# The sums of a block in two steps, and two loads of x asked for first, in a graph kernel with sorted edges

## The chip, the cores and the metric

The kernel runs on one core of a Trainium2 chip. Its time is what the device takes for one execution, in microseconds (us), and the time given is a median over several executions. A profile is one execution taken by the hardware profiler. PE is TensorE (matrix products), PEld its loading of weights, DVE is VectorE, ACT is ScalarE, POOL is GpSimd, SP is SyncE. SP, ACT and POOL also issue transfers (DMAs); on POOL these are the gathers, whose rows are picked by a list of indices.

## What is computed

One layer of a graph network over 12,500 nodes with 128 features and 412,500 edges, which come sorted by their target `dst`. Cut to what matters:

```python
theta = x[dst] - x[src]
w = sigmoid(relu(theta @ W1 + b1) @ W2 + b2)
agg = segment_sum(w * theta, dst)          # per node
indeg = segment_sum(1, dst)                # edges per node
y = x + agg + indeg * (x @ W4 + b4)
out = layernorm(y)                         # over the 128 features, no weights
```

Every edge has a gate `w` between 0 and 1. A node's result is the sum of its edges' gated differences, the number of its edges times a linear map of its own row, its own row, and a normalization.

## The kernel before

**The table.** Since `(x[dst] - x[src]) @ W1` is a difference of two rows of `x @ W1`, the kernel first makes a table `z` in DRAM whose rows are `x @ W1` and `x` side by side, 256 numbers. It does so in 14 chunks of up to 1024 rows: `table_load` (L726 to L731) asks for a chunk of x on ACT's queue, `table_chunk` (L734) turns it on PE (L743), copies it on ACT (L746), multiplies it by W1 (L749), copies that (L752) and x (L753) into a buffer, and SP writes the buffer to `z` (L754). Loads run up to two chunks ahead of the chunk worked on (`chunk`, L1243). The first two chunks are put behind `place_first_src` (L463), which turns the first list of `src` (load L164, copy L458, product L460, copy L464): `with after([first])` orders their instructions behind it.

**The sorting.** Edges are handled in parts of about 1400. For each set of parts a long generator, `place` (L481 on), sorts the edges of every part into places, most of it on DVE, and yields now and then, so that its steps can be spread between other work. It starts from the lists `es` and `ed` (SP's loads, L182) and ends with a list of rows to gather, `src_i`, copied by ACT (L687). The first set's loads are issued on SP near the start, and its steps are spread over the table's chunks and the first parts.

**A part and a block.** There are 300 parts (`s`), two to a block (`b`), 150 blocks; a block's targets lie in a window of 96 nodes. For part `s`:

- `gather(s)`: 8 gathers of 128 rows of `z` each, on POOL (L382), into one of 7 buffers (`zbuf`).
- `spread_y(s)`: products on PE that give each edge its target's row of `x @ W1` (L871). Later `y` tiles alternate between two.
- `logits(s)`, on DVE: subtract (L929), relu times W2 (L934), sum (L940), and the one-hot matrix of targets `ow` (L904).
- `open_gate`, `gate_sums` and `weigh`: the gate on ACT (L946, L952), then the gated rows `wx`, half on DVE (L974), half on ACT (`weigh_rest`, L981).

A few edges of each part, the "hot" ones, have their rows fetched in another way, by products with tables held in SBUF (`products_of_tiles`, L1035; `hot_rows(b)`, L1075 and L1079; `hot_logits`, L1088; `hot_weights`, L1099).

**The sums of a block.** `sums_of(b)` starts a tile in PSUM, `pa`, of which there is one, with the node's own part (L1132, L1133) and turns the next window (L794). `add_block(b)` (L1152) calls it and then adds on PE, all in `pa` (L1121): four wide products (260 columns) of the even part, four of the odd part, six narrow ones (130 columns) of the hot edges, and one that carries over the sums of the block before. `total(b)` copies parts of `pa` on ACT (L1169, L799), `finish(b)` adds the rest on DVE (L1180); `own` (L1188, L1190) and `normalize` (L1208 to L1233) make the output.

**The order of the work.** From part 18 on the order on PE, DVE and ACT is the order of the calls in `part(s)` (L1436 on). The queue of SP is in program order too; POOL's gathers follow one another in order. In `part(s)`, with `h` the part's number in its block, `logits(s)` comes first, then `spread_ahead(s)`, which issues `spread_y(s + 2)` and `gather(s + 3)`. That gather has a pace:

```python
paced[s + 3] = newest[0]
gather(s + 3)
```

`newest[0]` is the last product that `hot_rows`, `hot_products` or `products` put on PE, and the first of the part's gathers waits for it. With `h == 0` follows `add_block(b - 1)`, then in both parts `products_of_tiles`; with `h == 1` follows `hot_rows(b + 1)`. So the newest product before an even part is the last of `hot_rows`, and before an odd part the last of `products_of_tiles`. `total(b - 1)` and `finish(b - 1)` come with `h == 1`.

Of the kernel before, what the change touches and what calls it, by code (L numbers as in the profile page):

```python
# [81 lines left out]
def gnn_resnorm(  # L82
# [78 lines left out]
    def load_first(edges, s0, m):  # L161

        t = early(P, I32)[:m * K]
        nc.sync.dma_start(  # L164
            t, edges[s0 * BE:(s0 + m) * BE].rearrange("(p e) -> p e", e=P))
        return t
# [55 lines left out]
    load_bases(0, FIRST)  # L222
    wts = const.tile([P, 2, D], F32, name="wts")
    nc.sync.dma_start(wts[:, 0, :], W1)
    dst_f = load_first(dst, 0, FIRST)
    loaded = load(0)
    load_bases(FIRST, PLAIN)
# [101 lines left out]
        return nodes, (apart, most, area_c)  # L329


    wx_buf = [const.tile([P, K, AW], F32, name=f"wx{i}") for i in range(NW)]
    wxh_all = const.tile([P, 2 * SUB * HQ, AW], F32, name="wxh")
    wxh_buf = [wxh_all[:, i * SUB * HQ:(i + 1) * SUB * HQ, :] for i in range(2)]
    xT_all = const.tile([P, HX, HK], F32, name="xT")
# [13 lines left out]
    def pairs(s):  # L349
        return J if s < NF else JT  # L350
# [10 lines left out]
    def wx_of(s):  # L361

        if s < NH:
            return wxe_buf[s % 2]
        return wx_buf[s % (EW if s < PLAIN else NW)]
# [327 lines left out]
    with tc.manual_schedule(engines={SP}), tc.tile_pool(name="work", bufs=2) as wp, tc.tile_pool(  # L693
# [28 lines left out]
        def turning():  # L722

            return ps_l.tile([P, P * G], F32, name="pd")

        def table_load(c):  # L726
            n0, np_, m = chunks[c]
            xt = wx_buf[c % EW].rearrange("p k d -> p (k d)")[:, :BE]
            xt = xt.rearrange("p (t d) -> p t d", d=D)
            nc.scalar.dma_start(  # L730
                xt[:np_, :m, :], x[n0:n0 + np_ * m, :].rearrange("(p t) d -> p t d", t=m))  # L731
            return xt

        def table_chunk(c, xt):  # L734

# [173 lines left out]
        def logits(s):  # L909

            zs = rows_of(s)
            lg = parts[s]["lg"] = wp.tile([P, K, 1], F32, name="lg")
            y = parts[s]["y"]
            if s < NH:
                one_hot_w(s)
                for i, h in enumerate(y):
                    w2 = w2_r.rearrange("p (o d) -> p o d", o=1).to_broadcast([P, J, D])
                    nc.vector.scalar_tensor_tensor(h, h, 0.0, w2, op0=OP.max, op1=OP.mult)
                    nc.vector.tensor_reduce(lg[:, i * J:(i + 1) * J, 0], h, AX.X, OP.add)
                return  # L920
            h = zs[:, :, :D]
            n = pairs(s)
            half = h.rearrange("p (i k) d -> p i k d", i=2)[:, :, :n, :]
            if s < PLAIN:
                for i in range(2):
                    nc.vector.tensor_sub(half[:, i], y[i], half[:, i])
            else:
                yy = y[0][:, :n, :].rearrange("p (o k) d -> p o k d", o=1)
                nc.vector.tensor_sub(half, yy.to_broadcast([P, 2, n, D]), half)  # L929
            w2 = w2_b.rearrange("p (o d) -> p o d", o=1)  # L930
            n = K if s < NF else JT
            tiles = [slice(i, i + n) for i in range(0, K, J if n < K else K)]
            for at in tiles:
                nc.vector.scalar_tensor_tensor(  # L934
                    h[:, at, :], h[:, at, :], 0.0, w2.to_broadcast([P, n, D]),
                    op0=OP.max, op1=OP.mult)
            if s % SUB == 0:
                one_hot_w(s)
            for at in tiles:
                nc.vector.tensor_reduce(lg[:, at, 0], h[:, at, :], AX.X, OP.add)  # L940
            if s % SUB:
                one_hot_w(s)
# [175 lines left out]
        def products(to, terms, first, last):  # L1118

            for i, (one, w) in enumerate(terms):  # L1120
                newest[0] = nc.tensor.matmul(to if len(w.shape) == 3 else to[:, 0, :], one, w,  # L1121
                                             start=first and i == 0, stop=last and i == len(terms) - 1)

        def sums_of(b):

            pa = ps_l.tile([P, P * G], F32, name="pa")
            d = blocks[b]
            d["pa"] = pa[:WB, :2 * AW].rearrange("p (h c) -> p h c", h=2)
            d["pau"] = pa[:WB, AW:2 * AW + D]
            d["turned"] = pa[:, 2 * AW + D:2 * AW + D + WB]  # L1130
            u = pa[:WB, 2 * AW:2 * AW + D]
            nc.tensor.matmul(u, third, b4_t, start=True, stop=False)  # L1132
            nc.tensor.matmul(u, d["xuT"], wts[:, 1, :], start=False, stop=True)  # L1133
            if b + 1 < NK:
                turn(b + 1, d["turned"])

        def add_up(s, halves=(0, 1)):
# [11 lines left out]
            if end:  # L1149
                parts.pop(s)  # L1150

        def add_block(b):  # L1152

            sums_of(b)
            d = blocks[b]
            terms = []
            for s in range(b * SUB, b * SUB + SUB):
                wx = wx_of(s).rearrange("p (h k) d -> p k h d", h=2)
                terms += [(parts[s]["ow"][0][:, k, :], wx[:, k]) for k in range(pairs(s))]
                parts.pop(s)  # L1160
            terms += [(d["owh"][:, q, :], d["wxh"][:, q, :]) for q in range(SUB * HQ)]
            terms.append((d["sh"][:WB, :WB], carry[0][:WB, :AW]))
            products(d["pa"], terms, True, True)

        def total(b):

            d = blocks[b]
            a = d["a"] = carry[0] = wp.tile([P, AW + D], F32, name="a", bufs=3)
            nc.scalar.activation(a[:WB], d["pau"], AF.Copy)  # L1169
            d["u"] = a[:WB, AW:]  # L1170
            if b + 1 < NK:
                turned(b + 1, d["turned"])

        def finish(b):

            d = blocks[b]
            a = d["a"]
            plain = b * SUB < PLAIN
            if not plain:
                nc.vector.tensor_add(a[:WB, :AW], a[:WB, :AW], d["pa"][:, 0, :])  # L1180
# [57 lines left out]
            if b < NK:  # L1238
                load_block(b)

        xts, done = [], []

        def chunk():  # L1243
            c = len(done)
# [27 lines left out]
        def advance(kinds, n=1):  # L1272

            for _ in range(n):
                if steps[0] is None or steps[1] not in kinds:
                    return
                steps[1] = next(steps[0], None)
                if steps[1] is None:
                    steps[0] = None
# [148 lines left out]
        def spread_ahead(s):  # L1428

            if s + 2 < NS:  # L1430
                spread_y(s + 2)
                if PLAIN + AHEAD <= s + 3 < NS:
                    paced[s + 3] = newest[0]
                    gather(s + 3)

        def part(s):  # L1436

            b, h = divmod(s, SUB)
            credit[0] = min(credit[0] + 2.1, 5.0)
            if s in turns:  # L1440
                edges[s + 3] = turns[s], load(turns[s])
            if s in edges:
                i, loaded = edges.pop(s)
                assert steps[0] is None
                steps[:] = place(i, lambda: where[0](), *loaded), "k"
            for f in rest_of:
                if f[0] - 8 == s:
                    hot_load(f)
            if h == 0:
                fetch(b + 2)  # L1450
            if s == PLAIN:
                normalize(b - 2)
            done_b = h == 1 and PLAIN // SUB - 1 <= b - 1 < NK
            while opened:
                hot_out(*opened.pop(0))
            if h == 1:
                advance("c")
            if s < NS:
                logits(s)
            spread_ahead(s)  # L1460
            if h == 0 and PLAIN // SUB <= b - 1 < NK:
                add_block(b - 1)
            if tiled:
                products_of_tiles()
            if h == 1 and b + 1 < NK:
                hot_rows(b + 1)
            if s < NS:
                open_gate(s)
            if done_b:
                total(b - 1)  # L1470
            if s < NS:
                if h == 0:
                    hot_logits(b)
                else:
                    shift(b)
                weigh(s)
            if done_b:
                finish(b - 1)
            if h == 1:
                spend("kz", 1)  # L1480
            if h == 0 and b < NK:
                hot_weights(b)
            if s < NS:
                gate_sums(s)
            if done_b:
                own(b - 1)
            if s < NS:
# [215 lines left out]
```

## Time and profile before

| | us |
|---|---|
| median of 3 runs | 3143.19 (3138.27 to 3147.16) |
| the profiled execution | 3137.42 |
| its span | 3135.6 |
| PE, DVE, POOL, ACT busy | 2627.0, 2597.9, 2305.1, 2158.6 |
| POOL's gathers from `z` | 2250 by `src_i`, 112 by the first list |

The page gives, for each engine, its busy time and the number of instructions. A line of a group reads: line of the kernel, engine, operation, output and inputs, shapes, count, then busy time in us and the mean of one in ns, then the idle time of the engine just before these instructions, and what ended most of it. "issue" means that the engine waited for nothing that the profile shows. A line of the waits reads: engine, line and tile that waited, what for, us in total, how often, the longest. A line of the timeline reads: start and length in us, engine, line, operation, tiles, how many were merged, and in brackets the idle time before it with what ended it. A line of the stretches reads: from and to, length, busy us and count of PE, PEld, DVE, ACT and POOL, the clock granted to PE, the busy share of the DMA engines, and GB/s.

### The profile page before, as it was taken

The numbers are of one execution on the slowest core, as the hardware profiler recorded it, in microseconds if no ns is written. First come the engines' busy times: TensorE is split into PE (matmuls) and PEld (weight loads), VectorE is DVE, ScalarE is ACT, GpSimd is POOL, SyncE is SP. The second block draws the span as 40 slices with busy tenths as digits, with TensorE's granted clock in tenths as the row PEclk, the third lists the DMA queues.
The fourth block names the chain that finished last, engine by engine and source line by source line (L and its number), as shares of the span: only waits on it lengthen the run. The fifth ranks groups of instructions, "written<-read, shape, count | busy, mean of one in ns | idle before, by whom it ended". The sixth has DMA issues, their size and how long they took to land.

```text
span 3135.6 us, 52391 instructions
## 1 busy us (share of the span) xinstructions
PE 2627.0 (84%) x14981; PEld 2127.1 (68%) x14981; DVE 2597.9 (83%) x5715; ACT 2158.6 (69%) x5946; POOL 2305.1 (74%) x2403
## 2 busy tenths in 40 slices
PE   5859888888888888889888888897988888988887
PEld 4658676676767666677666666676766666776665
DVE  6797899888889888887798888976988888866666
ACT  5438777666776767677776676676776766777764
POOL 3675777777777777777777777777777777777774
PEclk8769999999999999999899998999899988999988
DMA  7555445455555555455555555554554454555543
GB/s 245 167 162 134 130 134 133 130 133 134 145 134 132 133 134 129 133 137 135 141 135 132 132 130 133 135 137 137 132 132 130 130 135 134 135 135 135 136 129 83
DMA packets 254642, 428.90 MB, mean 137 GB/s; under 512 B 72607, under 2 KB 172900, under 8 KB 252808
## 3 DMA queue, kind: packets, MB, share of 16 engines
q0 software_dynamic: 114400, 311.84, 35.9%
q1 hardware_dynamic: 137974, 107.23, 14.2%
q10 hardware_dynamic: 1970, 6.40, 0.6%
q8 instruction: 121, 1.98, 0.3%
q14 instruction: 177, 1.45, 0.2%
HBM read 404.34 MB, written 20.89 MB: 136 GB/s over the span
## 4 chain that ended last, share of the span: by engine, by line
DVE 28%; DMA 19%; PE 17%; ACT 15%; issue 12%; POOL 7%; DVEq 0%; SPq 0%; POOLq 0%; ACTq 0%
DMA zbuf<-z,src_i 17%; POOL zbuf L382 7%; DVE zbuf L929 6%; DVE zbuf L934 5%; DVE lg L940 5%; PE pa L1121 5%; PE pd L1035 3%; PE px L1075 2%; ACT of L1019 2%; DVE ow L904 2%; ACT wx L981 2%; PE y L871 2%; DVE hh L1088 2%; PE px L1079 2%; ACT of L1021 1%
## 5 line engine op out<-in xcount | busy, mean ns | idle before, releaser
L382 POOL DMA_INDIRECT zbuf<-z,src_i x2250 | 2162.9, 961 | 703.4 <-issue 440.7
L871 PE MATMUL y<-y,oh 64*128 64x128 f32 x2298 | 356.3, 300 | 366.3 <-DVE zbuf L929 243.3
L1121 PE MATMUL pa<-wx,ow 128*96 128x260 f32 (+1 forms) x2474 | 589.7, 395 | 0.0
L871 PEld LDWEIGHTS y<-y,oh 64*128 64x128 f32 x2298 | 300.1, 201 | 413.3 <-DVE zbuf L929 265.6
L1035 PE MATMUL pd<-of,tabs 128*128 128x128 f32 (+3 forms) x3468 | 521.1, 308 | 39.8 <-ACT xT L1049 39.6
L929 DVE TENSOR_TENSOR zbuf<-y,zbuf 128x1024 f32<-128x1024 f32 x282 | 343.8, 1219 | 213.3 <-DMA zbuf<-z,src_i 209.1
L1035 PEld LDWEIGHTS pd<-of,tabs 128*128 128x128 f32 x3468 | 476.1, 218 | 63.0 <-ACT xT L1049 49.8
L1121 PEld LDWEIGHTS pa<-wx,ow 128*96 128x96 f32 x2474 | 412.7, 177 | 126.8 <-issue 6.2
L1075 PE MATMUL px<-wni,xT 128*128 128x256 f32 x1128 | 419.7, 457 | 0.0
L946 ACT ACTIVATE fix<-lg,b_c 128x8 f32<-128x8 f32 x282 | 76.3, 271 | 468.4 <-DVE ow L904 298.8
L1019 ACT ACTIVATE of<-hot_src,nodes 128x384 f32<-128x384 f16 (+2 forms) x578 | 316.0, 593 | 117.4 <-PE pd L1035 117.4
L934 DVE SCALAR_TENSOR_TENSOR zbuf<-zbuf,fix 128x1024 f32<-128x1024 f32 (+1 forms) x297 | 360.6, 1214 | 10.1
L940 DVE TENSOR_REDUCE lg<-zbuf 128x8 f32<-128x1024 f32 (+1 forms) x297 | 358.6, 1208 | 5.4
L981 ACT ACTIVATE wx<-zbuf,wx 128x128 f32<-128x128 f32 x1124 | 357.1, 388 | 0.0
L1079 PEld LDWEIGHTS px<-y,oh 64*128 64x128 f32 (+1 forms) x1128 | 189.4, 198 | 172.7 <-issue 163.7
L1079 PE MATMUL px<-y,oh 64*128 64x128 f32 (+1 forms) x1128 | 275.0, 326 | 1.0 <-ACT oh L853 1.0
L974 DVE TENSOR_TENSOR wx<-zbuf,fix 128x512 f32<-128x512 f32 x282 | 193.2, 685 | 75.3 <-ACT fix L946 75.2
L1021 ACT ACTIVATE of<-of 128x768 f32<-128x768 f32 (+2 forms) x289 | 239.1, 827 | 9.2
L1075 PEld LDWEIGHTS px<-wni,xT 128*128 128x128 f32 x1128 | 190.3, 211 | 55.4 <-issue 9.4
L1121 PEld LDWEIGHTS pa<-wxh,owh 128*96 128x96 f32 x1692 | 202.9, 163 | 15.9
L1121 PE MATMUL pa<-wxh,owh 128*96 128x130 f32 x1692 | 211.2, 274 | 0.0
L904 DVE TENSOR_TENSOR ow<-fix,rel 128x384 f32<-128x384 f32 x318 | 173.1, 548 | 13.3 <-PE pa L1121 13.3
(301 smaller groups left out, 3997.3 us busy)
## 6 DMA issues: line engine op xcount, KB each, us to landing
zbuf<-z,src_i POOLq DMA_INDIRECT x2250
to_all<-off_d SPq DMA_DIRECT2D x282, 112.0 KB
hot_src<-hot_s SPq DMA_DIRECT2D x247, 96.0 KB
z<-zbuf SPq DMA_DIRECT2D x12, 1024.0 KB
xw<-in_x_dram SPq DMA_DIRECT2D x150, 48.0 KB
out_dram<-o SPq DMA_DIRECT2D x150, 48.0 KB
y<-z SPq DMA_DIRECT2D x294, 24.0 KB
wx<-in_x_dram ACTq DMA_DIRECT2D x12, 512.0 KB
```

The source lines that it names most:

```text
L382: ins = nc.gpsimd.indirect_dma_start(out=rows_of(s)[:, k, :], out_offset=None, in_=z if s >= NH else x, in_offset=IndirectOffsetOnAxis(ap= ...
L871: nc.tensor.matmul(y[:, j, :], d["oh"][:, (k0 + j) * P:(k0 + j + 1) * P], y_of(s), start=True, stop=True)
L929: nc.vector.tensor_sub(half, yy.to_broadcast([P, 2, n, D]), half)
L934: nc.vector.scalar_tensor_tensor(h[:, at, :], h[:, at, :], 0.0, w2.to_broadcast([P, n, D]), op0=OP.max, op1=OP.mult)
L940: nc.vector.tensor_reduce(lg[:, at, 0], h[:, at, :], AX.X, OP.add)
L981: nc.scalar.activation(wx[:, k, :D], rows_of(s)[:, k, D:], AF.Copy, scale=wx[:, k, D:D + 1])
L1019: nc.scalar.activation(of[:, t, :], hot_src[:, i % NU, :w], AF.Abs, bias=nodes[:, t:t + 1])
L1021: nc.scalar.activation(of, of, AF.Relu, scale=-1.0, bias=1.0)
L1035: newest[0] = nc.tensor.matmul(to[:, q], tabs[:, g * RG + q, t, :], of[:, t, q], start=t == 0, stop=t == HT - 1)
L1075: nc.tensor.matmul(to, xT[:, h, at], wni, start=True, stop=False)
L1079: newest[0] = nc.tensor.matmul(to[:, 0, :], oh[:, BP + q * P:BP + (q + 1) * P], y, start=False, stop=True)
L1121: newest[0] = nc.tensor.matmul(to if len(w.shape) == 3 else to[:, 0, :], one, w, start=first and i == 0, stop=last and i == len(terms) - 1)
```

## The change

Two edits, which do not depend on each other.

The first: `table_load` and its buffers move to the front of the program, and the first two chunks' loads of x are asked for there, on ACT's queue, in front of the loads of `dst` and of the lists for the sorting. They are no longer put behind `place_first_src`. The loads of the other chunks stay where they were.

The second: the sums of a block are made in two steps. `begin_block(b)`, in the odd part of block `b` behind `hot_rows(b + 1)`, starts `pa` and adds the four wide products of the block's even part. `add_block(b)`, in the next even part as before, adds the carried sums, the hot edges and the odd part. Since `pa` is one tile, `total(b - 1)` and `finish(b - 1)` move ahead of that: `total` in front of `logits(s)`, `finish` right behind it. What is computed is the same, and no instruction is added or removed.

```diff
+    wx_buf = [const.tile([P, K, AW], F32, name=f"wx{i}") for i in range(NW)]
+
+    def table_load(c):
...
+    xts = [table_load(c) for c in range(2)]
     dst_f = load_first(dst, 0, FIRST)
     loaded = load(0)
...
+        def terms_of(s):
+
+            wx = wx_of(s).rearrange("p (h k) d -> p k h d", h=2)
+            ow = parts.pop(s)["ow"][0]
+            return [(ow[:, k, :], wx[:, k]) for k in range(pairs(s))]
+
+        def begin_block(b):
+
+            sums_of(b)
+            products(blocks[b]["pa"], terms_of(b * SUB), True, False)
+
         def add_block(b):
 
-            sums_of(b)
             d = blocks[b]
-            terms = []
-            for s in range(b * SUB, b * SUB + SUB):
-                wx = wx_of(s).rearrange("p (h k) d -> p k h d", h=2)
-                terms += [(parts[s]["ow"][0][:, k, :], wx[:, k]) for k in range(pairs(s))]
-                parts.pop(s)
+            terms = [(d["sh"][:WB, :WB], carry[0][:WB, :AW])]
             terms += [(d["owh"][:, q, :], d["wxh"][:, q, :]) for q in range(SUB * HQ)]
-            terms.append((d["sh"][:WB, :WB], carry[0][:WB, :AW]))
-            products(d["pa"], terms, True, True)
+            terms += terms_of(b * SUB + 1)
+            products(d["pa"], terms, False, True)
...
-        xts, done = [], []
+        done = []
...
+            if done_b:
+                total(b - 1)
             if s < NS:
                 logits(s)
+            if done_b:
+                finish(b - 1)
             spread_ahead(s)
             if h == 0 and PLAIN // SUB <= b - 1 < NK:
                 add_block(b - 1)
...
             if h == 1 and b + 1 < NK:
                 hot_rows(b + 1)
+            if h == 1 and b < NK:
+                begin_block(b)
             if s < NS:
                 open_gate(s)
-            if done_b:
-                total(b - 1)
...
                 weigh(s)
-            if done_b:
-                finish(b - 1)
```

More of the change, by code (lines that the diff above doesn't have):

```diff
@@ L224, in gnn_resnorm @@
     nc.sync.dma_start(wts[:, 0, :], W1)
+    wx_buf = [const.tile([P, K, AW], F32, name=f"wx{i}") for i in range(NW)]
+    def table_load(c):
+        n0, np_, m = chunks[c]
+        xt = wx_buf[c % EW].rearrange("p k d -> p (k d)")[:, :BE]
+        xt = xt.rearrange("p (t d) -> p t d", d=D)
+        nc.scalar.dma_start(
+            xt[:np_, :m, :], x[n0:n0 + np_ * m, :].rearrange("(p t) d -> p t d", t=m))
+        return xt
+    xts = [table_load(c) for c in range(2)]
     dst_f = load_first(dst, 0, FIRST)
@@ L329, in constants @@
         return nodes, (apart, most, area_c)
-    wx_buf = [const.tile([P, K, AW], F32, name=f"wx{i}") for i in range(NW)]
     wxh_all = const.tile([P, 2 * SUB * HQ, AW], F32, name="wxh")
@@ L724, in turning @@
             return ps_l.tile([P, P * G], F32, name="pd")
[L726 to L732, printed above, removed]
         def table_chunk(c, xt):
```

## The prediction

> **What bounds the kernel now.** I read the busy shares first, then the POOL timeline and its groups, since every gather of rows of z is issued there, then the waits, then the stretches of the opening.
>
> ```profile
> PE 2627.0 (84%) x14981; PEld 2127.1 (68%) x14981; DVE 2597.9 (83%) x5715; ACT 2158.6 (69%) x5946; POOL 2305.1 (74%) x2403
> ...
> L382 POOL DMA_INDIRECT zbuf<-z,src_i x2172 | 2087.6, 961 | 661.7 <-issue 427.8 <-DMA zbuf<-z,src_i 46.0 <-ACT fix L946 38.7
> ...
> POOL zbuf L382 <- issue: 427.8, 1404, 0.3
> ...
> PE y L871 <- DVE zbuf L929: 243.3, 115, 6.8
> ```
>
> By the shares POOL looks free (74%). The group is POOL between 360 and 3108 us: 2172 gathers, 2087.6 us busy and 661.7 us idle, together 2749.3 us, the whole stretch of 2748. The waits of that stretch say that no wait was longer than 0.3 us: the idle time is the 0.30 us between one gather and the next. POOL issues one gather per 1.27 us without a hole, 8 per part, so a part costs 10.1 us whatever PE, DVE and ACT do inside it, as long as they keep up. PE's 243.3 us of waiting for DVE are slack, not loss. What can move the time is where this train begins and what follows its last gather.
>
> ```profile
> 95.71 0.94 POOL L382 DMA_INDIRECT zbuf<-z,src  x1 [5.46 <-issue]
> ...
> 247.63 0.94 POOL L382 DMA_INDIRECT zbuf<-z,src_i  x1 [5.59 <-ACT src_i L687]
> ...
> 297.85 0.94 POOL L382 DMA_INDIRECT zbuf<-z,src_i  x1 [10.52 <-ACT wx L981]
> ...
> 309.55 0.94 POOL L382 DMA_INDIRECT zbuf<-z,src_i  x1 [2.00 <-issue]
> ...
> 329.56 0.94 POOL L382 DMA_INDIRECT zbuf<-z,src_i  x1 [0.30 <-issue]
> ...
> 350.78 0.94 POOL L382 DMA_INDIRECT zbuf<-z,src_i  x1 [1.01 <-PE pz L1079]
> ...
> 371.82 0.95 POOL L382 DMA_INDIRECT zbuf<-z,src_i  x1 [0.30 <-issue]
> ...
> 3107.38 0.95 POOL L382 DMA_INDIRECT zbuf<-z,src_i  x1 [0.30 <-issue]
> ```
>
> These are the first gathers of parts 4, 18, 22, 23, 25, 27 and 29, and the last gather of all. The train stalls at 95.71 (the table z must be whole), at 247.63 (the first sorted list), at 297.85, 309.55 and 350.78 (the matmul that paces the gather), and never again. So the time is the start of part 27's gathers (350.78), plus 2757.5 us of issue to 3108.3, plus 27.3 us of tail to the span's 3135.6. The execution's own time is 3137.42; the median of the runs shown is 3143.19, 5.8 us above it.
>
> **The change, part by part.**
>
> First, the two x loads. Before, they stand behind the first placing of src and in a queue of waits.
>
> ```profile
> 2.65 0.31 ACT L458 ACTIVATE tabs<-tabs 128x128 f32<-128x128 int32 x1 [0.62 <-DMA tabs<-in_src_dram]
> ...
> 3.00 1.15 SPq L182 DMA_DIRECT2D es<-in_src_dram  x2
> ...
> 3.58 0.28 ACT L464 ACTIVATE src<-px 128x128 int32<-128x128 f32 x1 [0.62 <-PE px L460]
> ...
> 4.20 1.24 SPq L182 DMA_DIRECT2D ed<-in_dst_dram  x2
> ...
> 6.10 5.94 ACTq L730 DMA_DIRECT2D wx<-in_x_dram  x3
> ...
> 8.72 0.16 DVE L499 TENSOR_TENSOR col<-ed 128x1 f32<-128x1 int32 x1 [3.63 <-DMA ed<-in_dst_dram]
> ...
> 11.82 1.08 PE L743 MATMUL px<-wni,wx 128*128 128x128 f32 x4 [8.27 <-DMA wx<-in_x_dram]
> ...
> 12.94 0.60 ACT L746 ACTIVATE xT<-px 128x512 f32<-128x512 f32 x1 [9.08 <-PE px L743]
> ...
> 15.46 1.06 ACT L753 ACTIVATE zbuf<-wx 128x1024 f32<-128x1024 f32 x1 [0.97 <-DMA wx<-in_x_dram]
> ...
> 20.64 6.37 SPq L754 DMA_DIRECT2D z<-zbuf  x2
> ```
>
> Three loads are issued from 6.10 on, although L464, behind which they are put, ends at 3.86. The first matmul on x begins at 11.82, 5.72 us after the issue. In the changed program two loads head ACT's queue, so they go out about when SP's first do (under 1 us). With the same 5.72 us the first transpose could begin at 6.5, 5.3 us earlier; it cannot begin before L464's end at 3.86, 8.0 earlier. But the third load stays in front of ACT's first copy (L746), and in the new order of the DMA semaphores it waits for the first es load. Loads of this kind took 8.72 - 4.20 = 4.5 us from issue to use, so es, issued at 3.00, is there at 7.5. L746 then runs at about 8.0 instead of 12.94: 4.9 us earlier. The 0.97 us wait at 15.46 goes too, but a later x load, in front of ACT's next copy, now waits for the load of W2, which is not earlier, so I count 5.0. The bounds: 0, if other queues give it back, and 4.9 + 0.97, rounded up to 6, if they do not.
>
> What it is moved past: SP's first loads (src, W1, dst, es, ed). Two loads of 512 KB share the DMA engines with them.
>
> ```profile
> 0.00:5.00 5.00, 0.44 (x1) 0.18 (x1) 3.43 (x35) 1.87 (x3) 2.02 (x10) 1.00 0.26 69
> 5.00:10.00 5.00, 0.00 (x0) 0.00 (x0) 1.37 (x9) 0.00 (x0) 3.08 (x4) 1.00 0.92 241
> ...
> 40.00:70.00 30.00, 16.06 (x108) 13.06 (x107) 28.81 (x68) 18.10 (x30) 10.85 (x11) 0.87 0.95 325
> ...
> 26.34 0.17 DVE L422 COPY xT<-px 128x16 f32<-128x16 f32 x1 [7.79 <-PE px L420]
> ```
>
> In the first 5 us the DMA engines are 26% busy, in the next 5 at 92%: the loads move into idle time. At 241 GB/s, 1 MB takes 4.4 us; that is the most by which the sort's lists can come later, and DVE has 7.79 us of waiting in front of L422 to cover it. In the Trainium skill, "DMA: Bandwidth & Descriptors", section "Queues, rings and completion order", says that each DMA engine serves its queues in turn, a packet at a time. By that rule src would land later by a few packets and not behind the whole megabyte; no run here shows it yet.
>
> Does the gain reach part 4's gathers at 95.71? Loads of x and writes of z follow chunk by chunk in one chain. From 40 to 70 us the DMA engines are 95% busy, but with the same bytes begun earlier they also end earlier. SP reaches its first z write only at 20.64, behind its small loads, and the second z write waits for ACT, so the first gives less than the second. Placing the first list is spread over the chunks and moves with them. From 95.71 to 247.63 POOL is fed by what came before, and the stalls at 247.63 and 297.85 end with parts that started earlier. Taken: -5.0, between -6 and 0.
>
> Second, the sums. No instruction is added or removed; begin_block takes three small products and 4 of the 8 wide ones of a block from the even part to the end of the odd part before it. Their price:
>
> ```profile
> 325.42 0.38 PE L1079 MATMUL pz<-y,oh 128*128 128x128 f32 x2
> 325.87 1.16 PE L871 MATMUL y<-y,oh 64*128 64x128 f32 x8
> 326.95 0.26 PE L1132 MATMUL pa<-b_t,third 65*96 65x128 bf16 x1
> ...
> 327.38 3.67 PE L1121 MATMUL pa<-wx,ow 128*96 128x260 f32 x16
> ...
> 367.08 0.38 PE L1079 MATMUL pz<-y,oh 128*128 128x128 f32 x2
> ```
>
> From 326.95 to 327.38 are 0.43 us for the small ones, half of 3.67 is 1.84: 2.3 us per block. Over some 136 blocks (2172 gathers, 16 to a block) this shifts work inside PE's slack: nothing, while POOL is the bound. If the cover were gone, it would be 0 in PE-bound stretches too, as the sum over a block is the same.
>
> It does move one thing, the pace. gather(s + 3) of an even s waits for the newest product on PE. That was the last of hot_rows (L1079); it becomes the last of begin_block, 2.3 us later. Part 27's gathers stand right behind L1079 (1.01 us of waiting), and by the same line of the code part 23's (2.00). Both then start 2.3 us later; not twice, since the POOL train shifts once. Part 25's have slack: L1079 ended at 325.80, the gather began at 329.56, 3.8 us. Part 29's: 367.46 to 371.82, 4.4 us. Both exceed 2.3, so they are free. Taken: +2.3. The bounds: 0, if PE's waits ahead of those points swallow it, and twice that, 4.6, if PE's products run there at half their speed.
>
> Third, total before logits and finish before weigh. ACT's two copies (L1169, L799) go in front of the gate's L946, DVE's L1180 in front of L974. Inside the train it is free. At the end it counts:
>
> ```profile
> 3102.18 0.36 ACT L1169 ACTIVATE a<-pa 96x258 f32<-96x258 f32 x1
> ...
> 3102.58 0.36 ACT L1115 ACTIVATE sh<-lag,step_c 96x96 f32<-96x96 f32 x1
> ...
> 3120.15 0.42 DVE L974 TENSOR_TENSOR wx<-zbuf,fix 128x256 f32<-128x256 f32 x1 [0.67 <-ACT fix L946]
> ...
> 3120.59 0.29 DVE L1180 TENSOR_TENSOR a<-a,pa 96x130 f32<-96x130 f32 x1
> ...
> 3120.93 0.34 PE L1132 MATMUL pa<-b_t,third 65*96 65x128 bf16 x1 [2.31 <-DVE a L1180]
> ```
>
> 0.4 us of copies (3102.18 to 3102.58) leave the chain, and L1180 fits partly into the 0.67 us wait. The last block's sums, begun at 3120.93 behind L1180, still run on PE after it, since pa has one buffer: splitting them does not shorten the tail. Taken: -0.5, between -2.3 (half a block's sums out of the tail) and 0.
>
> There is one new wait. begin_block writes pa, of which there is one, so PE waits for L1180 of the block before, and for ACT's copies in front of it; queued behind on PE is the next part's spread, and DVE waits for that.
>
> ```profile
> L934 DVE SCALAR_TENSOR_TENSOR zbuf<-zbuf,fix 128x1024 f32<-128x1024 f32 (+1 forms) x297 | 360.6, 1214 | 10.1
> L940 DVE TENSOR_REDUCE lg<-zbuf 128x8 f32<-128x1024 f32 (+1 forms) x297 | 358.6, 1208 | 5.4
> L974 DVE TENSOR_TENSOR wx<-zbuf,fix 128x512 f32<-128x512 f32 x282 | 193.2, 685 | 75.3 <-ACT fix L946 75.2
> ...
> 321.07 0.48 PE L1079 MATMUL px<-y,oh 64*128 64x128 f32 x2
> ```
>
> Both engines go on from the end of the subtraction L929: DVE has L934, L940 and one short instruction to L1180, about 3 us; PE has the spread (1.16) and hot_rows (321.07 to 325.80, 4.7), 5.9 us. So L1180 is done first, and I take 0; its price, if not, is the last rival.
>
> Sum: -5.0 + 2.3 - 0.5 = -3.2 us on 3137.42, 3134.2; carried to the median shown, 3140.0. What a measurement of this kernel can tell from no change is 0.3%, 9.4 us.
>
> **Rivals.**
>
> *The opening gives nothing back* (chance 0.14): the DMA-bound stretch 40 to 70 us (95%) swallows it. For it: SP's z writes start at 20.64 with or without the loads. Against: 0.26 busy in the first 5 us. Then 0 + 2.3 - 0.5 = +1.8: 3145.0. The change would not do what its second half says.
>
> *The opening gives more* (0.18): the sort's chain also starts earlier by more than the table does, and part 18's stall of 5.59 us at 247.63 goes. Then -6 - 5.6 + 0 to 2.3 - 0.5, at most -12.1: 3131.1. For it: DVE is 28.81 of 30 us busy from 40 to 70. Against: the next stall, 10.52 us at 297.85, is of PE's pace and would take the gain.
>
> *Another engine is the bound* (0.03). If it were PE, work moved in front of its waits would fill them: of the 243.3 us for DVE about half lies in front of even parts, -120 us, 3023. If it were DVE, L1180 would fill the 75.2 us of waiting in front of L974, at most with its own 0.29 x 136 = 39 us, 3104. Against both: POOL without a hole. The Trainium skill, "Perfetto Trace Analysis", section "Identifying the Most-Contended Engine", takes the engine of highest occupancy for the bound, and for TensorE the share of weight loads. That would name DVE (83%) and not POOL (74%). Here the 0.3 us between gathers decide against it: they are not counted as busy, and with them POOL is full.
>
> *Slower* (0.17): the one pa. If PE, behind hot_rows, had to wait for L1180 at every block, the spread would come late, then DVE, then the gathers. Two parts of POOL are 20.2 us; PE's work in a block is 84% of that, 17.0, so it decides from a stall of 3.2 us per block on. At 3.3 us: 0.1 x 136 = +14 us on the forecast, 3154. For it: before, sums_of had half a block of room between finish and its first product, now a few us. Against: the 3 us and 5.9 us above.
>
> **How the numbers follow.** The forecast has 0.48; its own range is -6 + 0 - 2.3 to 0 + 4.6 + 0, 3135 to 3148. With the first rival 0.62 lie within 0.3%. Faster: 0.18 + 0.03 = 0.21. Slower: 0.17. The whole range takes in the second rival (3131) and the last (3154) with a few us for the runs' own spread (3138.27 to 3147.16 before): 3128 to 3156.
>
> **What would show it.** Right: the first L743 near 6 us, L746 near 8, part 4's gathers near 91, part 27's near 348, behind a product of begin_block (L1121's line), no POOL gap over 0.3 us after that, tail 26.8 us. Wrong: L746 still near 13; POOL gaps in the train; PE waiting at L1132 for L1180.

## The result, and the profile after

The changed kernel takes 3132.36 us (median of 17 runs), the kernel before 3140.21 us (17 runs beside them): ratio 0.9974, 95% interval 0.9964 to 0.9983, so 8.2 us less (5.3 to 11.3). The forecast was 3.2 us less. The direction is right, the size is not: some 5 us come from a place that the prediction called free. One of the 17 runs took 3207.53 us at a granted clock of 0.745, against 0.90 to 0.91 in the others, and the ratio leaves it out.

The profiled execution of the changed kernel took 3140.64 us (span 3138.9), 8 us above its own median and longer than the one of before (3137.42). So the two profiles cannot be subtracted; each step has to be looked at where it acts. From the timeline of the changed kernel (ACT and its queue, then PE, then POOL):

```profile
0.75 0.87 ACTq L231 DMA_DIRECT2D wx<-in_x_dram  x2
...
5.77 0.28 ACT L474 ACTIVATE src<-px 128x128 int32<-128x128 f32 x1 [0.63 <-PE px L470]
7.56 0.34 ACTq L231 DMA_DIRECT2D wx<-in_x_dram  x1
7.94 0.60 ACT L748 ACTIVATE xT<-px 128x512 f32<-128x512 f32 x1 [1.89 <-DMA es<-in_src_dram]
```
```profile
6.11 1.12 PE L745 MATMUL px<-wni,wx 128*128 128x128 f32 x4 [0.37 <-ACT src L474]
```
```profile
100.17 0.94 POOL L392 DMA_INDIRECT zbuf<-z,src  x1 [4.97 <-issue]
...
314.69 0.95 POOL L392 DMA_INDIRECT zbuf<-z,src_i  x1 [4.13 <-issue]
...
355.92 0.95 POOL L392 DMA_INDIRECT zbuf<-z,src_i  x1 [0.98 <-PE pa L1123]
```

The loads leave at 0.75 instead of 6.10, the first product on x runs at 6.11 instead of 11.82 and ACT's first copy at 7.94 instead of 12.94, behind the third load, which waits for es. The price is seen too: L474 (L464 before) ends 2.2 us later, half of the 4.4 us that the prediction gave as the most. Then the lead is lost: part 4's gathers start at 100.17 (before 95.71), part 27's at 355.92 (before 350.78).

The waits between 360 and 3108 us of the changed kernel (engine, line, what for, us in total, times, longest) and one group of that stretch:

```profile
POOL zbuf L392 <- issue: 423.8, 1390, 0.3
...
DVE a L1188 <- ACT xuT L801: 8.7, 8, 2.1
DVE wx L976 <- ACT fix L948: 7.3, 7, 1.3
```
```profile
L1134 PE MATMUL pa<-b_t,third 65*96 65x128 bf16 x136 | 30.3, 222 | 0.0
```

POOL's train has no hole here either. PE never waits for `pa` (0.0 us ahead of L1134). DVE, which in the same stretch of before waited 68 us for the gate ahead of the weighing (L974, now L976), does finish's L1188 in that time and waits 7.3 us:

```profile
DVE wx L974 <- ACT fix L946: 68.2, 147, 3.9
```

What that does to POOL is the subject of the experiments.

### The profile page after: what moved, and what is told of

Read it like the earlier page. It is cut to its first block, busy times and chain, and to the rows that moved or that the text cites. A ratio compares the mean times of both kernels' runs of the same rounds, so it can differ in the third digit from the quotient of the medians.

```text
span 3138.9 us, 52351 instructions
## 1 busy us (share of the span) xinstructions
PE 2645.3 (84%) x14981; PEld 2142.4 (68%) x14981; DVE 2600.5 (83%) x5715; ACT 2157.8 (69%) x5946; POOL 2305.6 (73%) x2403
## 4 chain that ended last, share of the span: by engine, by line
DVE 27%; PE 20%; DMA 19%; issue 14%; ACT 12%; POOL 7%; DVEq 0%; SPq 0%; ACTq 0%; POOLq 0%
DMA zbuf<-z,src_i 17%; POOL zbuf L392 7%; DVE zbuf L931 6%; DVE zbuf L936 5%; PE pa L1123 5%; PE pd L1037 4%; PE px L1077 3%; ACT wx L983 3%; DVE lg L942 2%; PE y L873 2%; DVE ow L906 2%; DVE hh L1090 2%; PE px L1081 2%; DVE wx L976 2%; ACT of L1021 2%
## 5 line engine op out<-in xcount | busy, mean ns | idle before, releaser
L873 PE MATMUL y<-y,oh 64*128 64x128 f32 x2298 | 366.7, 305 | 374.0 <-DVE zbuf L931 359.3
L873 PEld LDWEIGHTS y<-y,oh 64*128 64x128 f32 x2298 | 307.7, 205 | 452.6 <-DVE zbuf L931 383.2
L1123 PE MATMUL pa<-wx,ow 128*96 128x260 f32 (+1 forms) x2474 | 582.3, 381 | 0.0
L1037 PE MATMUL pd<-of,tabs 128*128 128x128 f32 (+3 forms) x3468 | 544.4, 317 | 20.0 <-ACT xT L1051 19.5
L1037 PEld LDWEIGHTS pd<-of,tabs 128*128 128x128 f32 x3468 | 508.9, 226 | 56.1 <-ACT xT L1051 27.5
L1123 PEld LDWEIGHTS pa<-wx,ow 128*96 128x96 f32 x2474 | 388.2, 170 | 96.7 <-issue 0.8
L1077 PE MATMUL px<-wni,xT 128*128 128x256 f32 x1128 | 426.9, 464 | 0.0
L936 DVE SCALAR_TENSOR_TENSOR zbuf<-zbuf,fix 128x1024 f32<-128x1024 f32 (+1 forms) x297 | 360.6, 1214 | 10.1
L976 DVE TENSOR_TENSOR wx<-zbuf,fix 128x512 f32<-128x512 f32 x282 | 193.2, 685 | 28.4 <-ACT fix L948 9.7
L1123 PEld LDWEIGHTS pa<-wxh,owh 128*96 128x96 f32 x1692 | 196.0, 163 | 0.0
L1094 ACT ACTIVATE wxh<-lgh,b_c 128x6 f32<-128x6 f32 x141 | 42.8, 304 | 211.2 <-DVE hh L1090 211.2
```

Source lines behind the costliest of these rows:

```text
L873: nc.tensor.matmul(y[:, j, :], d["oh"][:, (k0 + j) * P:(k0 + j + 1) * P], y_of(s), start=True, stop=True)
L936: nc.vector.scalar_tensor_tensor(h[:, at, :], h[:, at, :], 0.0, w2.to_broadcast([P, n, D]), op0=OP.max, op1=OP.mult)
L976: nc.vector.tensor_tensor(wx, xs, w.to_broadcast(list(xs.shape)), op=OP.mult)
L1037: newest[0] = nc.tensor.matmul(to[:, q], tabs[:, g * RG + q, t, :], of[:, t, q], start=t == 0, stop=t == HT - 1)
L1077: nc.tensor.matmul(to, xT[:, h, at], wni, start=True, stop=False)
```

## The experiments

Kernels that are compared ran on one chip in turn with the kernel before. "Train" is the time from part 27's first gather to the end of the last, 2178 gathers. Four chips came up in these runs. On two of them the kernel before took 3142 and 3145 us, on the other two 3827 and 3731 us; these are kept apart.

### One half at a time

`again` is the changed kernel itself. `loads` has the first half alone, `sums` the second alone:

```diff
 loads, against the kernel before
+    xts = [table_load(c) for c in range(2)]
     dst_f = load_first(dst, 0, FIRST)
...
-        xts, done = [], []
+        done = []
```
```diff
 sums, against the changed kernel
-    xts = [table_load(c) for c in range(2)]
     dst_f = load_first(dst, 0, FIRST)
...
-        done = []
+        xts, done = [], []
```

> The changed kernel once more, for a second profile and more times. If the time is the start of the train of gathers (part 27's first gather) plus a fixed 2757 + 27 us, then this profile's execution time minus part 27's start is again 2784 to 2786 us, whatever the start is, and the start lies below the 355.92 us of the first profile, near 348. If instead the train itself varies from run to run, the difference moves by several us while the start stays near 356.

> The first half alone: two loads of x at the front, sums as before. My sum gives -5.0 us (-6 to 0) against before, with the first x product near 6 us and part 4's gathers near 91. The rival, that the table's later chunks or the stages behind the table swallow the lead, gives 0 (within 2 us) and part 4's gathers at 95 or later.

> The second half alone: sums in two steps, loads as before. My sum gives +2.3 - 0.5 = +1.8 us (-2 to +4) against before, and part 27's gathers behind a product of begin_block. If the gain of about 8 us that was measured comes from here and not from the loads, this kernel gains 5 to 10 us and the loads alone gain nothing.

Measured against 3142.45 us for before (32 runs): `again` 3134.09, ratio 0.9974 (0.9957 to 0.9990); `loads` 3136.53, 0.9992 (0.9978 to 1.0006), 2.5 us less with an interval that takes in zero; `sums` 3135.22, 0.9990 (0.9977 to 1.0003), 3.1 us less, as wide. The plain medians lie 5.9 and 7.2 us below before; the intervals belong to the ratios. Times alone don't tell the halves apart. The profile of `again` answers its question in part: the train begins at 347.54 us, near the 348 expected, but the execution's 3127.77 us less that start are 2780.2 and not 2784 to 2786. So the train is not fixed. Here is the group of the train's gathers, taken from the first to the last of the 2178, in before, loads, again and sums:

```profile
L382 POOL DMA_INDIRECT zbuf<-z,src_i x2178 | 2094.3, 962 | 664.3 <-issue 429.0 <-DMA zbuf<-z,src_i 46.0 <-ACT fix L946 38.7
```
```profile
L392 POOL DMA_INDIRECT zbuf<-z,src_i x2178 | 2093.5, 961 | 664.3 <-issue 438.1 <-DMA zbuf<-z,src_i 41.7 <-ACT fix L948 39.9
```
```profile
L392 POOL DMA_INDIRECT zbuf<-z,src_i x2178 | 2086.5, 958 | 664.3 <-issue 438.1 <-DMA zbuf<-z,src_i 42.7 <-ACT fix L948 39.6
```
```profile
L382 POOL DMA_INDIRECT zbuf<-z,src_i x2178 | 2086.0, 958 | 664.2 <-issue 443.6 <-DMA zbuf<-z,src_i 40.8 <-ACT fix L946 38.4
```

The idle time between gathers is the same to 0.1 us. The gathers themselves are 8 us shorter in all in the two with the sums in two steps, and the train falls from 2757.5 and 2756.7 to 2749.7 and 2749.2 us. The first profile of the changed kernel, with the same sums as `again`, seems to speak against it, with a train of 2755.9 us:

```profile
L392 POOL DMA_INDIRECT zbuf<-z,src_i x2178 | 2092.1, 961 | 664.8 <-issue 425.0 <-DMA zbuf<-z,src_i 46.0 <-ACT fix L948 36.3
```

The next section takes the gathers apart and shows why.

### Which gathers are shorter, and why

Most gathers take 0.945 us; 81 to 92 of a train take over 1 us and are called long here. What the long ones take over 0.945 us, and the mean of all others, by kernel:

| kernel | finish moved | long | their excess, us | the others, mean ns | train, us |
|---|---|---|---|---|---|
| before | no | 92 | 34.0 | 946.0 | 2757.5 |
| loads | no | 92 | 34.1 | 945.5 | 2756.7 |
| finish3 | yes | 83 | 27.4 | 947.5 | 2754.6 |
| changed | yes | 83 | 26.5 | 948.5 | 2755.9 |
| again | yes | 87 | 26.7 | 945.8 | 2749.7 |
| sums | yes | 81 | 26.4 | 945.6 | 2749.2 |
| pace | yes | 84 | 25.9 | 946.0 | 2749.4 |
| pace2 | yes | 89 | 28.6 | 945.6 | 2751.4 |

In all six profiles with finish moved the long gathers lose 5.4 to 8.1 us less than in before. In two of them, the changed kernel's first and `finish3`, the other gathers are slower by 2.5 and 1.5 ns each, evenly over the train, which makes 5.3 and 3.2 us and hides much of the gain. `again` is the same kernel as the first of these and is not slower, so this is not of the change; where it comes from is open.

One of the long gathers, on POOL and on DVE of the kernel before, and the same sorting step in `again` (whose train began 3.2 us earlier):

```profile
419.16 1.68 POOL L382 DMA_INDIRECT zbuf<-z,src_i  x1 [0.30 <-ACT sh L1115]
```
```profile
418.33 0.69 DVE L974 TENSOR_TENSOR wx<-zbuf,fix 128x512 f32<-128x512 f32 x1 [0.34 <-ACT fix L946]
418.93 0.28 DVE L1180 TENSOR_TENSOR a<-a,pa 96x130 f32<-96x130 f32 x1
419.13 0.88 DVE L556 SCALAR_TENSOR_TENSOR ew<-ew 128x702 f32<-128x702 f32 x1
```
```profile
415.90 0.95 POOL L392 DMA_INDIRECT zbuf<-z,src_i  x1 [0.30 <-ACT fix L948]
417.15 0.95 POOL L392 DMA_INDIRECT zbuf<-z,src_i  x1 [0.30 <-ACT fix L1198]
```
```profile
415.59 0.29 DVE L1188 TENSOR_TENSOR a<-a,pa 96x130 f32<-96x130 f32 x1 [2.11 <-ACT xuT L801]
415.80 0.68 DVE L976 TENSOR_TENSOR wx<-zbuf,fix 128x512 f32<-128x512 f32 x1
416.40 0.88 DVE L566 SCALAR_TENSOR_TENSOR ew<-ew 128x702 f32<-128x702 f32 x1
```

In before the sorting step L556 starts 0.03 us ahead of a gather and ends at 420.01; the gather ends at 420.84, 0.83 us later. Over all gathers of the train that it lengthens the same holds: a gather that starts while L556 runs ends 0.81 to 0.83 us after L556 does, nearly as if it began anew there. Of 62 gathers that started under an L556, more than 0.13 us before its end, 61 were lengthened, by 26.5 us in all, out of the 34.0 us that the long gathers lose. In `again` finish's L1188 no longer stands between the weighing and the sorting step. The gather of the same number starts at 415.90, ahead of the step; the first one under the step is the next, 0.13 us before the step's end, and it is not longer. This step comes 0.5 us later against the gathers than in before, since DVE had waited 2.11 us for ACT; most come earlier, as follows.

Counted over the whole train: in before and `loads` 20 of the 92 sorting steps stand directly behind finish, and each of these 20 lengthened a gather, by 8.5 and 8.4 us in all. With finish moved, the 20 steps stand behind the weighing, and 12 to 14 of them lengthen one, by 3.0 to 4.2 us, in all six profiles with the move (changed kernel, `again`, `sums`, both of the pace, `finish3`). That is 4.3 to 5.5 us. In each of these 16 to 18 of the 20 steps come earlier against the gather, most often by 0.2 us. From the step's start to the next gather's there are 0.33 and 0.34 us (median of the 20) in before and `loads`, 0.54 to 0.65 in the six. The step takes 0.88 us, so more of it is over when the gather starts. All other long gathers together lose 0.2 to 2.8 us less in the six, and 0.2 more in `loads`; which steps give that was not followed up.

The Trainium skill, "SBUF — State Buffer", section "SBUF: two separate sides", says that VectorE and GpSimd share one pair of ports under an exclusive lock, and that the one that comes second waits for the whole instruction of the first. The waits under L556 agree with it. It also counts every VectorE instruction with two inputs in SBUF in against a GpSimd instruction that reads SBUF; there the trace agrees too. 234 gathers of before started under L934 and 128 under L974, and none was long. Both of these take one input from `fix`, which the kernel keeps in PSUM (L274 and L275), and so have only one in SBUF:

```python
cps = ctx.enter_context(tc.tile_pool(name="ps_c", bufs=1, space=bass.MemoryType.PSUM))
fix = cps.tile([P, 512], F32, name="fix")
```

L556 reads `ew` twice, from SBUF. Under four other sorting steps with both inputs in SBUF (L534, L540, L542, L543) 9 gathers of before started, and all 9 were long. The lock is seen one way only: 58 steps L556 began while a gather was running, and none of them took over 0.92 us.

### Finish alone

```diff
+            if done_b:
+                total(b - 1)
             if s < NS:
                 logits(s)
+            if done_b:
+                finish(b - 1)
             spread_ahead(s)
...
-            if done_b:
-                total(b - 1)
...
-            if done_b:
-                finish(b - 1)
```

> The kernel before with total and finish moved ahead, for the third time. Where the kernel before takes about 3142 us: train 2749 us instead of 2757, 7 to 9 us less in long gathers, time 6 to 9 us below before. Where it takes 3.73 to 3.83 ms there is no train without holes, and I expect no change within 0.3%, as in finish2.

`finish3` took 3140.14 us against 3145.09 (23 runs): 0.9980 (0.9965 to 0.9994), 6.3 us less. Its train:

```profile
L382 POOL DMA_INDIRECT zbuf<-z,src_i x2178 | 2091.0, 960 | 664.7 <-issue 433.2 <-DMA zbuf<-z,src_i 44.8 <-ACT fix L946 38.7
```

2754.6 us, 2.9 less than before and not the 8 that I expected. But its long gathers lose 27.4 us instead of 34.0, 6.6 less, of which the steps behind finish gave 4.3; that is as much as with the sums in two steps (5.4 to 8.1). The train is longer by the 3.2 us of its other gathers. So moving finish, with the sums in one step, shortens the long gathers by itself, and the split sums are not needed for it.

The first two runs of this kernel came on the other chips:

> The kernel before with one edit: total and finish of a block move in front of logits and right behind it, as in the change; sums in one step, loads as before. By my prediction this is free inside the train of gathers and gives -0.5 us at the end. By the theory the first four runs suggest, it gives nearly all that the sums gave: the sorting step L556 that stood directly behind finish's L1180 on DVE then starts some 0.3 to 0.5 us earlier against the gathers, the long gathers (over 1.0 us) lose 7 to 9 us in all, the train from part 27's first gather to the last gather's end falls from 2757 to about 2749 us, and the time by 6 to 9 us. If the new place of the products does it, the train stays at 2755 or above.

`finish`: 3817.96 against 3826.83 us, 0.9973 (0.9952 to 0.9994).

> The kernel before with total and finish moved ahead, once more, because in the run called finish the kernel before itself took 3826 us and the gathers of all kernels stopped at every part, behind loads of SP's queue, so that no train was there to measure. Where the kernel before takes about 3142 us again, I expect the same as there: a train of about 2749 us instead of 2757, 7 to 9 us less in long gathers, and a time 6 to 9 us below before. If the new place of the products makes the gain, the train stays at 2755 or above and the time within 2 us.

`finish2`: 3727.04 against 3730.53 us, 0.9995 (0.9981 to 1.0009). On both, POOL stops ahead of nearly every part and there is no train to shorten. From part 27 on the long gathers of `finish` lose 20.6 us against 12.7 in `before2` on the same chip: the place that helps in a train need not help without one. Why `finish` was still 10 us faster (2 to 18) is open.

### The pace

```diff
         def begin_block(b):
 
+            last = newest[0]
             sums_of(b)
             products(blocks[b]["pa"], terms_of(b * SUB), True, False)
+            newest[0] = last
```

> The changed kernel, with one difference: the pace of the gathers asked for in an even part stays on the last product of hot_rows and not on the last of begin_block. My term of +2.3 us says that this is 2.3 us faster than the changed kernel (0 to 4.6), with part 27 no longer waiting. If the pace at parts 23 and 27 is not what sets the start of the train, it is the same as the changed kernel within 1.5 us.

> The changed kernel with the pace of the gathers left on the last product of hot_rows, once more. Where the kernel before takes 3.73 to 3.83 ms (granted clock 0.81 to 0.84), the run again2 showed POOL waiting 110 times for a product of begin_block, 651 us in all between 500 and 3500, where the kernel before waits 311 us for hot_rows. If the pace behind begin_block is what costs the change 10% there, this kernel is within 2% of before; if the earlier finish or the split of the products costs it, it is 8 to 10% slower like the change. Where the kernel before takes about 3142 us, I expect 10 to 13 us less than before, as in the first run of it.

`pace`: 3128.70 us, 0.9963 (0.9949 to 0.9977). `pace2`, on the chip of `finish3`: 3137.78, 0.9980 (0.9967 to 0.9993). Around the changed kernel's 0.9974 these say nothing clear. The trace does show the step: part 23's gathers wait 2.00 to 2.02 us in before, `loads`, `finish3` and `pace2`, and 4.13 to 4.16 in the changed kernel, `again` and `sums`, 2.15 us more (`pace` itself is the exception, with 6.13). Part 27's wait stays at 1.0 to 1.1 us, outside the two runs of the pace (1.70 and 1.38): the shift comes once. `pace2` came on a chip where the question of its expectation, what the pace costs at a low clock, did not arise; it stays open.

### Where PE is slower

> The changed kernel once more. Where the kernel before takes about 3142 us, it is a third profile: train 2749 to 2756 us, time 8 us below before. Where the kernel before takes about 3826 us, it tells whether the change itself is what made the two kernels built on it 6.5 and 8.4% slower there: if so, it is 5 to 8% slower than before too; if those came from their own edits, it is within 1%.

`again2`, on the chip of `finish2`: 4110.41 us against 3730.53, ratio 1.1032 (1.1000 to 1.1065). The change that gains 0.26% on one chip costs 10% on another. Cores and POOL's waits of `finish2` and of `again2`:

```profile
core 0: 3727.3 us, clock 0.835
```
```profile
POOL zbuf L382 <- PE pz L1079: 301.6, 136, 5.2
POOL zbuf L382 <- remote: 269.3, 124, 2.8
```
```profile
core 0: 4105.3 us, clock 0.793
```
```profile
POOL zbuf L392 <- PE pa L1123: 815.6, 134, 9.4
...
POOL zbuf L392 <- remote: 152.4, 86, 3.0
```

The granted clock is 0.84 and 0.79, against 0.90 to 0.92 where the train runs. Here the gathers of nearly every second part wait for PE's pace: 136 times for hot_rows with finish moved, 134 times for begin_block in the changed kernel, and 6.1 us each instead of 2.2. Together with the waits for which the profile names no releaser that is 968 us against 571, 397 more, close to the 380 by which the kernel is longer. `finish2` has the moved finish and costs nothing, so it is the split of the sums with its pace (or, less likely, the loads). That the pace alone does it is argued from these waits; the run that was to show it met another chip. A rival stands beside it: with the split sums the granted clock itself is lower, 0.790 against 0.836 on this chip (means over the runs), and 0.905 in `again` and `sums` against 0.912 in before and `loads`. PE was busy for 3009.2 us instead of 2851.0 with the same number of products, so up to 158 of the 380 us may be slower products and not their new place. Whether the waits lower the clock or the clock makes the waits was not tried.

### The step twice, and fewer gathers

```diff
 twice, against the changed kernel
                 v.scalar_tensor_tensor(left, left, float((HR - r + 1) * AREA), left,
                                        op0=OP.is_lt, op1=OP.mult)
+                v.scalar_tensor_tensor(left, left, float((HR - r + 1) * AREA), left,
+                                       op0=OP.is_lt, op1=OP.mult)
```
```diff
 fewer, against the changed kernel
-        for k in slots(s):
+        for k in slots(s)[:7] if 32 <= s < 296 and s % 4 == 0 else slots(s):
```

> The changed kernel, with the sorting step L566 (702 numbers, both inputs in SBUF) issued twice in a row; the second leaves its input as it is. If a gather that starts while this instruction runs has to wait for its end, the long gathers' excess rises by 19 us or more (as much again as L566 costs now, up to 70 us if nothing fits between the two) and the time with it. If DVE and POOL do not touch, the 92 more instructions of 0.89 us lie in DVE's slack and the time stays within 3 us.

> The changed kernel with one of the eight gathers left out in every fourth part from 32 to 292 (66 gathers; those rows keep what an earlier part left there). If POOL's train of gathers sets the time, it falls by 66 x 1.25 = 83 us (75 to 90). If PE or DVE is the bound, by under 20 us.

Both ran where before took 3826.83 us: `twice` 4149.90, 1.0844 (1.0801 to 1.0886); `fewer` 4078.05, 1.0652 (1.0611 to 1.0692). `fewer` leaves 66 gathers out, whose rows keep what an earlier part left there, and that can hardly cost 6.5%. Both are built on the changed kernel, and what their times show is most likely its loss on such a chip, as in `again2`. Neither the doubled sorting step nor the missing gathers were measured in a train, and what 66 gathers are worth stays open. The profiles still say something of the doubled step. From part 27 on 67 of 75 gathers that started under it were lengthened, by 26.5 us, against 48 of 56 and 16.0 us in `fewer` with the step once, on the same chip; again they end 0.82 us after the step. All long gathers together lose 37.1 us against 23.1. More of the step makes more of the loss, though less than the 19 us expected, which were meant for a train.

> The kernel before, for a second profile. If the length of its train is a property of the order of its instructions, the train is again 2755 to 2759 us with 34 to 39 us of excess in long gathers, and only its start differs (345 to 357). If the length varies from run to run, it may come out at 2750.

`before2` took 3817.17 us (clock 0.810) and had no train either.

## Why the prediction was right and wrong

**POOL is the bound.** Right on the chips of the first measurements: no hole in the train of the changed kernel, nor in `finish3`. The sentence that a part costs 10.1 us "whatever PE, DVE and ACT do inside it" was wrong: DVE's sorting steps lengthen gathers while DVE keeps up. That on the chips with a lower granted clock POOL stops at nearly every part falls under the sentence's own condition, "as long as they keep up". One row was misread: the stall at 297.85 is put to PE's pace, while the row names ACT's `wx` (L981); no term of the sum hangs on it.

**The loads, -5.0 us.** The steps came as forecast: L745 at 6.11 (near 6), L748 at 7.94 (near 8) behind es. How much arrives at part 4 depends on PE's speed while the table is made, which differs from run to run. PE runs a group of 8 products with W1 in 2.07 or in 1.16 us; of the 24 groups, 3 to 15 were slow. Two groups of the changed kernel's first profile, and two of `again` at about the same time:

```profile
40.74 2.07 PE L751 MATMUL pz<-wts,xT 128*128 128x128 f32 x8 [0.69 <-ACT xT L748]
...
51.76 1.16 PE L751 MATMUL pz<-wts,xT 128*128 128x128 f32 x8 [0.75 <-ACT xT L748]
```
```profile
38.24 1.16 PE L751 MATMUL y<-wts,xT 128*128 128x128 f32 x8 [1.27 <-ACT xT L748]
40.58 1.16 PE L751 MATMUL y<-wts,xT 128*128 128x128 f32 x8 [0.74 <-ACT xT L748]
```

| kernel | x loads in front | slow groups | part 4 | part 27 |
|---|---|---|---|---|
| before | no | 6 | 95.71 | 350.78 |
| sums | no | 7 | 99.33 | 356.48 |
| finish3 | no | 9 | 98.72 | 353.67 |
| pace2 | yes | 3 | 90.56 | 344.98 |
| again | yes | 4 | 90.52 | 347.54 |
| loads | yes | 7 | 94.23 | 345.07 |
| pace | yes | 8 | 95.39 | 356.22 |
| changed | yes | 15 | 100.17 | 355.92 |

With 7 to 9 slow groups the loads in front make part 4 start at 94.2 and 95.4 instead of 99.3 and 98.7, 4.2 us earlier: near the size of the forecast, once runs of like PE speed are compared. That the slow groups make the difference is argued from this table, with one profile each. `loads` as a whole gained 2.5 us with an interval from -6.9 to +1.9.

**The pace, +2.3 us.** Part 23 waits 2.15 us more; part 27 not once more. Right on these chips. The sentence of the step before, that the shifted products would cost nothing "in PE-bound stretches too, as the sum over a block is the same", did not hold in `again2`: the sum of the work is the same, but the gathers wait behind it, 815.6 us in all, at a clock of 0.79.

**Total and finish earlier.** This is the step that failed. "Inside the train it is free" priced it by DVE's and ACT's slack. DVE's slack was real; what was not seen is that the place of a DVE instruction decides which sorting step meets which gather. The long gathers lose 5.4 to 8.1 us less where finish is moved, and the train is 1.7 to 8.3 us shorter, instead of 0. The tail, for which I took -0.5 us from 27.3, came out between 26.7 and 28.7 in the seven profiles, no change.

**The sum.** -4.2 for the loads, +2.15 for part 23 and -1.7 to -8.3 for the train (2757.5 against 2749.2 to 2755.9) make -3.8 to -10.4 us. The measured -8.2 (-11.3 to -5.3) lies in it. The loads and the pace alone, the prediction's own terms, make some -2 of it. In absolute terms 3132.36 lies just below the forecast's own range of 3135 to 3148 and inside the whole one of 3128 to 3156. That one was so wide for two rivals whose mechanisms did not come, so that the time lies in it is in part luck. The evidence against myself stood in the profile of before: a mean gather of 961 ns, where nearly every row of the timeline says 940 to 950.

**The rivals.** An opening that gives nothing back: not in the profiles, where 4.2 us reach part 4; the times of `loads` alone do not rule it out. The single `pa`: no wait for it at L1134, as argued. Part 18's stall of 5.59 us: 5.58 in `again`, 2.33 in the first profile and 3.24 in `loads`, so it shrank in some and went in none. Another engine as the bound: not where the forecast was made, but the slow side of that rival is what happened on the chips with the lower clock, at 10% and not at 0.4%; that PE bounds it there is argued from the waits.

## What to carry to other kernels

When an engine issues at a fixed beat and never waits, look at the longest of its instructions before calling the others' work free: their excess, and what runs on the neighbour at that moment, is the cost that the waits don't list. Here it came from DVE instructions with both inputs in SBUF; those with one input in PSUM cost POOL nothing. A pace that is tied to "the newest product" moves whenever products move, and slack of a few us on one chip may be none on another. A change of 0.3% measured on one chip should be tried on a second, since here the same edit was worth -0.26% and +10.3%.

## What the runs showed of the hardware

- A gather that starts while the sorting step L556 runs, a DVE instruction with both inputs in SBUF, ends 0.82 us after the step's end: up to 0.74 us lost each, 26.5 us in the train of before. Under DVE instructions with one input in PSUM (L929, L934, L974: 595 gathers) none was long.
- PE ran 8 products of the table in 1.16 or in 2.07 us. The first faster group came between 12.7 and 51.8 us, and from 63 to 72 us on one to five were slow again in every profile of the table above. The column of the granted clock shows 1.00 for a stretch of the changed kernel in which every group was slow:

```profile
20.00:40.00 20.00, 15.70 (x63) 13.15 (x63) 14.66 (x42) 10.88 (x22) 5.65 (x6) 1.00 0.69 243
```

- The same kernel took 3142, 3145, 3731 and 3827 us on four chips; the granted clock was 0.912 in the first profile of before and 0.810 in `before2`. With the sums in two steps the clock was lower than before on each of the chips where both ran (0.905 to 0.912, 0.790 to 0.836). What limits the kernel on the slower chips was not settled: the profile of `before2` puts 24% of the chain to a releaser that it cannot name:

```profile
PE 36%; another core or an unknown queue 24%; ACT 22%; DVE 9%; issue 7%; DMA 1%; POOL 1%; DVEq 0%; SPq 0%; ACTq 0%; POOLq 0%
```
